# Running the last 64 rows of two products in pairs on the two halves of the partitions, with biases added by ScalarE and GpSimd

## The chip, the cores and the metric

One core of a Trainium2 chip runs the kernel. TensorE multiplies matrices into PSUM banks, VectorE, ScalarE and GpSimd (DVE, ACT and POOL in the profile) work on rows of 128 partitions, and SyncE (SP) issues the DMA transfers. The metric is the device time of one execution in microseconds.

## What is computed

Input x has 8 batches of 512 tokens of 576 numbers, all f32. A first layer rotates x in a 64-dimensional subspace; a second is one transformer block whose attention runs over the 16 heads of one token, and whose shifts, scales and gates come from a condition vector of each batch.

```
x = x + ((x U) R - x U) U^T                    # U from a QR, R = expm of a skew matrix
shift_a, scale_a, gate_a, shift_m, scale_m, gate_m = split(silu(c) @ ada_w + ada_b, 6)
h = layernorm(x) * (1 + scale_a) + shift_a
q, k, v = split((h @ qkv_w + qkv_b), 3)        # 576 -> 3 * 576; per token 16 heads of 36
att = softmax(q k^T / 6) v                     # 16 x 16 scores for each token
x = x + gate_a * (reshape(transpose(att)) @ proj_w + proj_b)
h = layernorm(x) * (1 + scale_m) + shift_m
x = x + gate_m * (gelu(h @ fc1_w + fc1_b) @ fc2_w + fc2_b)      # 576 -> 2304 -> 576
```

## The kernel before

A preparation stage (about 240 us, its order written out by hand) makes U by a QR on VectorE, the rotation by a matrix exponential on TensorE and GpSimd, and the modulation tables. The exponential's products (`products`, L367) take 64x64 blocks alternately from partitions 0-63 and 64-127. `mod` holds shift and scale with features on partitions.

The main part goes over 17 units of the tokens: two of one 128-token tile and 15 of two tiles. A contraction over 576 features is cut into chunks of 128, 128, 128, 128 and 64 rows (`KROWS`). The last chunk has a 65th row: `xn`, the normed tile, is padded with a column of ones (`padded`, L577), which transposed becomes a row of ones, and the weights carry the bias as row 576. `srows(c)` is 65 for the last chunk. So the query product and fc1 get their bias inside the last matmul.

- `normed` (L600): layer norm on VectorE, with the root taken by GpSimd (L610).
- `feature_major` (L663) and `Projection.turn_normed` (L803): TensorE transposes normed tiles; ScalarE scales and shifts them on the way out of PSUM into `hT` or `h2T` (L675, L814).
- `qkv` (L685): for a token tile, four groups of 432 columns, five chunks each, into one bank of the pool `ps_mm` (two banks); ScalarE copies each group to `tok` (L703).
- `attention` (L708): VectorE multiplies (L721, L743) and sums (L727, L749) per four heads; ScalarE takes the exponential.
- `Projection.product` (L786): attention's output by proj_w into `ps_mm`; VectorE multiplies by the gate and so frees the bank (L795, `pt`), then adds.
- `norm` (L798): normed again, then GpSimd adds `gb2` (gate_m times fc2's bias, made once a batch at L1007 from `b2`, which stays in SBUF) to the tile (L801).
- `fc1` (L829): for group g of 9, two blocks k of 128 hidden features. Each has its own weight tile w1 (320 KB, pool `wst`, ring of 4) and five chunks (L838) into one half of a bank of `ps_f1` (two banks). One gelu takes the whole bank (L846).
- `mlp` (L907): fc2 by a Strassen-like scheme with seven products instead of eight. GpSimd makes sums of gelu's output (L923 to L926), weights come from `in_fc_q` (wq) and from combinations made during the first batch (`comb_d`, wt). Its matmuls are at L938 to L943, one product left for the end at L953. The first batch uses `mlp_plain` (L893).

In the unit loop (from L1000), the queries of unit k+1 are issued during unit k: three groups, then the turn of attention's output, then the fourth group, the projection, the second tile's groups, the turn of the normed tile, then the MLP. In a batch's second unit the next batch's rotation is set between fc1 groups (`aside`); it begins with `gps` (L631), a 64-row product. In fc1's loop fc2 runs one group behind: fc1(g), fc2(g-1), fc1(g+1). At a batch's first unit `gate_rows` (L597) loads the gates by DMA.

Outside the preparation a scheduler orders the instructions of each engine at compile time by its own estimate of when each is ready; each engine and SP then works its list in order.

Of the kernel before, what the change touches and what calls it, by code (L numbers as in the profile page):

```python
# [9 lines left out]
F32 = mybir.dt.float32  # L10
# [38 lines left out]
def rotate_then_dit_block(  # L49
# [7 lines left out]
    qkv_w: bass.AP,  # L57
    proj_w: bass.AP,
    fc1_w: bass.AP,
    fc2_w: bass.AP,  # L60
    fc2_q: bass.AP,
    fc2_b: bass.AP,
# [5 lines left out]
    def load_rows(dst, src, tail):  # L68

        nc.sync.dma_start(out=dst[:, 0:4], in_=src[0:512].rearrange("(c p) n -> p c n", p=128))  # L70
        nc.sync.dma_start(out=dst[0:tail, 4], in_=src[512 : 512 + tail])
# [22 lines left out]
    nc.gpsimd.memset(u[R:, 4, 0:R], 0.0)  # L94
    fmi = const.tile([128, B // 2, R], F32, tag="fmi", name="fmi")
    mod = const.tile([128, 4, NK, B], F32, tag="mod", name="mod")
    b2 = const.tile([128, D], F32, tag="b2", name="b2")

    wqkv = const.tile([128, NK, 3 * D], F32, tag="wqkv", name="wqkv")

    t3 = const.tile([128, NP, HALF], F32, tag="t3", name="t3")

    def srows(c):
        return 65 if c == 4 else 128


    for i in range(4):
        nc.gpsimd.memset(mod[64:65, i, 4, :], float(i % 2))


    xin = ctx.enter_context(tc.tile_pool(name="xin", bufs=1))
# [2 lines left out]
    with tc.manual_schedule(engines=engines), tc.tile_pool(name="prep", bufs=1) as prep, tc.tile_pool(name="qrs", bufs=2) as qrs, tc.tile_pool(  # L114
# [202 lines left out]
        def modulation(v):  # L317
            ps = ps_m.tile([128, NK, B], F32, tag="m", name=f"mod_{v}")
            for c, rows in enumerate(KROWS):
                first = v * D + c * 128  # L320
                nc.tensor.matmul(
                    ps[0:rows, c], lhsT=ada_rows[:, first : first + rows], rhs=ident[0:B, 0:B], start=True, stop=True
                )
            for c0, c1, rows in ((0, 4, 128), (4, 5, 64)):
                dst = mod[0:rows, v // 3 * 2 + v % 3, c0:c1, :]
                if v % 3:
                    nc.scalar.activation(dst, ps[0:rows, c0:c1], AF.Identity, bias=ones[0:rows, 0:1])
                else:
                    nc.scalar.copy(dst, ps[0:rows, c0:c1])


        wr = prep.tile([128, NK, NSKEW], F32, tag="wr", name="wr")
# [142 lines left out]
        for j in range(R):  # L475
            t, done = qr_step(j, t, done)
            if j > 1:
                next(side, None)
            if j == 8:
                load_rows(wqkv, qkv_w, 65)  # L480
                nc.sync.dma_start(out=b2, in_=fc2_b.to_broadcast([128, D]))
                for g in (6, 7, 8):
                    load_ada(g)
        for _ in side:
# [92 lines left out]
    def padded(tag, n):  # L577
        out = []
        for k in range(n):
            t = big.tile([128, NK * 128], F32, tag=f"{tag}{k}", name=f"{tag}{k}")  # L580
            nc.gpsimd.memset(t[:, D:], 0.0)
            nc.gpsimd.memset(t[:, D : D + 1], 1.0)
            out.append(t)
        return out

    xns = padded("xn", 5)
    ats = padded("at", 2)
    turn = {"xn": 0, "at": 0}

# [10 lines left out]
    def normed(xt, name):  # L600

        st = small.tile([128, 2, 6], F32, tag="st", name=f"st_{name}")
        mv = small.tile([128, 2], F32, tag="mv", name=f"mv_{name}")
        rs = small.tile([128, 1], F32, tag="rstd", name=f"rstd_{name}")
        xn = take("xn", xns)
        for n in range(2):
            nc.vector.bn_stats(st[:, n, :], xt[:, n * HALF : (n + 1) * HALF])
        nc.vector.bn_aggr(mv, st)
        nc.vector.tensor_scalar(rs, mv[:, 1:2], LN_EPS, None, ALU.add)  # L609
        nc.gpsimd.tensor_tensor(rs, rs, mhalf[:, 0:1], ALU.pow)  # L610
        nc.vector.tensor_scalar(xn[:, 0:D], xt, mv[:, 0:1], rs, ALU.subtract, ALU.mult)
        return xn

    hTs = {}
# [48 lines left out]
    def feature_major(b, half):  # L663

        if half == 0:
            hTs[b] = big.tile([128, NK, S], F32, tag="hT", name=f"hT_{b}")
        hT = hTs[b]

        pair = normed_x.pop((b, half))
        for c in range(NK):  # L670
            rows = srows(c)
            ps = ps_mm.tile([128, 2, 128], F32, tag="mm", name=f"htr_{b}_{half}_{c}")
            for t in range(2):
                nc.tensor.transpose(ps[:, t, :], pair[t][:, c * 128 : (c + 1) * 128], ident)
            nc.scalar.activation(  # L675
                hT[0:rows, c, half * 256 : half * 256 + 256],
                ps[0:rows].rearrange("p t s -> p (t s)"),
                AF.Identity,
                bias=mod[0:rows, 0, c, b : b + 1],
                scale=mod[0:rows, 1, c, b : b + 1],  # L680
            )

    toks = {}
# [1 line left out]
    def qkv(b, i):  # L685


        hT = hTs[b]
        tok = tiles.tile([128, 3 * D], F32, tag="qkv", name=f"qkv_{b}_{i}", bufs=3)
        N = 3 * D // 4  # L690

        def group(n):
            ps = ps_mm.tile([128, N], F32, tag="mm", name=f"qkvp_{b}_{i}_{n}")
            for c in range(NK):
                k = srows(c)
                nc.tensor.matmul(  # L696
                    ps,
                    lhsT=hT[0:k, c, i * 128 : (i + 1) * 128],
                    rhs=wqkv[0:k, c, n * N : (n + 1) * N],
                    start=c == 0,  # L700
                    stop=c == NK - 1,
                )
            nc.scalar.copy(tok[:, n * N : (n + 1) * N], ps)  # L703

        toks[b, i] = tok
        return [lambda n=n: group(n) for n in range(4)]

    def attention(b, ts):  # L708
# [3 lines left out]
        NU = len(ts)  # L712
        hb = f"{b}_{ts[0]}"
        own = [toks.pop((b, i)) for i in ts]
        sc2 = small.tile([128, 2, H, H], F32, tag="sc", name=f"sc_{hb}", bufs=2)[:, 0:NU]
        for t, tok in enumerate(own):
            q = tok[:, 0:D].rearrange("p (h d) -> p h d", d=DH)
            k = tok[:, D : 2 * D].rearrange("p (h d) -> p h d", d=DH)
# [37 lines left out]
    class Projection:  # L756
# [46 lines left out]
        def turn_normed(self, cs):  # L803

            if cs[0] == 0:
                self.h2T = tiles.tile([128, NK, 256], F32, tag="h2T", name=f"h2T_{self.hb}", bufs=1)
            b, tokens = self.b, len(self.ts) * 128
            ps = ps_f1.tile([128, 2, 2, 128], F32, tag="f1", name=f"h2tr_{self.hb}_{cs[0]}")
            for k, c in enumerate(cs):
                for t in range(len(self.ts)):  # L810
                    nc.tensor.transpose(ps[:, k, t, :], self.xn[t][:, c * 128 : (c + 1) * 128], ident)
            for k, c in enumerate(cs):
                rows = srows(c)
                nc.scalar.activation(  # L814
                    self.h2T[0:rows, c, 0:tokens],
                    ps[0:rows, k].rearrange("p t s -> p (t s)")[:, 0:tokens],
                    AF.Identity,
                    bias=mod[0:rows, 2, c, b : b + 1],
                    scale=mod[0:rows, 3, c, b : b + 1],
                )  # L820


# [5 lines left out]

    def fc1(pr, g):  # L829

        hb, h2T, NU = pr.hb, pr.h2T, len(pr.ts)
        ps = ps_f1.tile([128, 2, NU * 128], F32, tag="f1", name=f"fc1_{hb}_{g}")
        for k in range(2):
            w1 = wst.tile([128, NK, 128], F32, tag="w1", name=f"w1_{hb}_{g}_{k}")
            nc.sync.dma_start(out=w1, in_=fc1_w[2 * g + k])
            for c in range(NK):
                n = srows(c)
                nc.tensor.matmul(  # L838
                    ps[:, k],
                    lhsT=w1[0:n, c, :],  # L840
                    rhs=h2T[0:n, c, 0 : NU * 128],
                    start=c == 0,
                    stop=c == NK - 1,
                )
        gt = tiles.tile([128, 2, NU, 128], F32, tag="gt", name=f"gt_{hb}_{g}", bufs=3)
        nc.scalar.activation(gt.rearrange("p k t s -> p (k t s)"), ps.rearrange("p k s -> p (k s)"), AF.Gelu)  # L846
        return gt

    def finish(hb, t, n, made, gate):
# [139 lines left out]
    def now(pieces):  # L989
        for piece in pieces:  # L990
            piece()
# [11 lines left out]
    for k, (b, ts) in enumerate(units):  # L1003
        if ts[0] == 0:
            gate_a, gate_m = gate_rows(0, b), gate_rows(1, b)
            gb2 = big.tile([128, D], F32, tag="gb2", name=f"gb2_{b}")
            nc.gpsimd.tensor_tensor(gb2, gate_m, b2, ALU.mult)  # L1007

        pr = Projection(b, ts, gate_a)
        if k == 0:  # L1010
# [5 lines left out]
            q = qkv(nb, nts[0]) + qkv(nb, nts[1])  # L1016
        if len(ts) == 1:
            pr.turn(0)
            now(q[:1])
            pr.product(0, 0)  # L1020
            pr.product(0, 1)
            pr.norm(0, gb2)
            now(q[1:3])
            pr.turn_normed((0, 1))
            now(q[3:])
        else:
            now(q[:3] if k > 2 else q)
            pr.turn(0)
            now(q[3:4] if k > 2 else [])
            pr.product(0, 0)  # L1030
            pr.turn(1)
            pr.product(0, 1)
            pr.norm(0, gb2)
            pr.product(1, 0)
            pr.product(1, 1)
            pr.norm(1, gb2)
            now(q[4:7] if k > 2 else [])
            pr.turn_normed((0, 1))
            now(q[7:] if k > 2 else [])
# [64 lines left out]
```

## Time and profile before

| | us |
|---|---|
| median of 3 runs (2232.11 to 2236.47) | 2233.76 |
| profiled execution | 2228.81 |
| its span, first to last instruction | 2227.0 |
| preparation, up to | 240 |
| a steady unit of two tiles (1203 to 1320) | 117 |
| TensorE, VectorE busy in it | 116.5, 95.3 |
| fc1 group, two tiles (20 matmuls) | 4.32 |

PE is the matmuls, PEld the weight loads. A group of instructions in the profile is a line, an engine, an operation, its tiles and form, a count, then busy time, mean ns of one, and idle time before them with what ended it. A timeline row is start, length, engine, line, operation, tiles, form and count; neighbours of one kind are merged. Successive matmuls overlap in the records, since the end of each is modelled: what one costs is the step from its start to the next one's. SPq rows are DMA issues.

### The profile page before, as it was taken

The numbers are of one execution on the slowest core, as the hardware profiler recorded it, in microseconds if no ns is written. First come the engines' busy times: TensorE is split into PE (matmuls) and PEld (weight loads), VectorE is DVE, ScalarE is ACT, GpSimd is POOL, SyncE is SP. The second block draws the span as 40 slices with busy tenths as digits, with TensorE's granted clock in tenths as the row PEclk, the third lists the DMA queues.
The fourth block names the chain that finished last, engine by engine and source line by source line (L and its number), as shares of the span: only waits on it lengthen the run. The fifth ranks groups of instructions, "written<-read, shape, count | busy, mean of one in ns | idle before, by whom it ended". The sixth has DMA issues, their size and how long they took to land.

```text
span 2227.0 us, 26157 instructions
## 1 busy us (share of the span) xinstructions
PE 2104.2 (94%) x9571; PEld 1570.8 (71%) x9571; DVE 1789.4 (80%) x2443; ACT 386.7 (17%) x817; POOL 679.6 (31%) x846
## 2 busy tenths in 40 slices
PE   7788879899799999999999999999999999999998
PEld 3485437666568686868687777777786868686877
DVE  8997399899678797969796979697988889697930
ACT  2232111122021111111111112121211122111110
POOL 2151000113434242424242433324332334242422
PEclk9755789999999999999999999999999999999999
DMA  9101116743647373845565465637373737364654
GB/s 304 30 2 62 50 54 206 249 124 111 186 156 233 107 214 108 251 128 170 155 201 165 153 178 168 205 116 208 128 231 98 215 114 225 111 202 122 200 178 125
DMA packets 211698, 347.58 MB, mean 156 GB/s; under 512 B 82382, under 2 KB 100123, under 8 KB 211572
## 3 DMA queue, kind: packets, MB, share of 16 engines
q1 hardware_dynamic: 211572, 345.92, 51.3%
q8 instruction: 77, 1.26, 0.2%
q14 instruction: 49, 0.40, 0.1%
HBM read 313.46 MB, written 32.39 MB: 155 GB/s over the span
## 4 chain that ended last, share of the span: by engine, by line
PE 65%; DVE 14%; issue 11%; DMA 6%; POOL 3%; ACT 1%; SPq 0%; POOLq 0%; DVEq 0%; ACTq 0%
PE fc L838 26%; PE fc L938 8%; PE qkvp L696 7%; PE fc L943 5%; DVE sc L727 3%; PE fc L940 3%; PE p L953 3%; DMA w<-in_fc_w 3%; PE fc L893 2%; PE ada L310 2%; DMA out<-x 1%; DVE qk L721 1%; PE zps L640 1%; DVE pv L743 1%; DVE att L749 1%
## 5 line engine op out<-in xcount | busy, mean ns | idle before, releaser
L838 PE MATMUL fc<-h2T,w 128*128 128x256 f32 (+3 forms) x3060 | 656.4, 368 | 2.0 <-ACT h2T L814 1.9
L838 PEld LDWEIGHTS fc<-h2T,w 128*128 128x128 f32 (+1 forms) x3060 | 549.4, 191 | 76.8 <-ACT h2T L814 7.0
L696 PE MATMUL qkvp<-wqkv,hT 128*128 128x432 f32 (+1 forms) x1280 | 480.9, 529 | 1.3 <-DVE pt L795 0.9
L721 DVE TENSOR_TENSOR qk<-qkv 128x2304 f32<-128x2304 f32 x128 | 327.3, 2557 | 122.9 <-ACT qkv L703 120.4
L696 PEld LDWEIGHTS qkvp<-wqkv,hT 128*128 128x128 f32 (+1 forms) x1280 | 240.6, 191 | 204.5 <-issue 196.4
L743 DVE TENSOR_TENSOR pv<-sc,qkv 128x2304 f32<-128x2304 f32 x128 | 330.9, 2585 | 3.3
L749 DVE TENSOR_REDUCE att<-pv 128x144 f32<-128x2304 f32 x128 | 326.5, 2551 | 3.3
L727 DVE TENSOR_REDUCE sc<-qk 128x64 f32<-128x2304 f32 x128 | 326.3, 2549 | 2.8
L923 POOL TENSOR_TENSOR ss<-gt 128x128 f32<-128x128 f32 x126 | 135.1, 1072 | 539.4 <-ACT gt L846 539.4
L846 ACT ACTIVATE gt<-fc 128x512 f32<-128x512 f32 (+1 forms) x153 | 87.5, 572 | 725.2 <-PE fc L838 725.0
L703 ACT COPY qkv<-qkvp 128x432 f32<-128x432 f32 x128 | 66.3, 518 | 559.0 <-PE qkvp L696 552.6
L943 PEld LDWEIGHTS fc<-wt,ss 128*128 128x128 f32 x1008 | 140.5, 190 | 13.2
L943 PE MATMUL fc<-wt,ss 128*128 128x144 f32 x1008 | 144.1, 286 | 0.0
L938 PE MATMUL fc<-wq,gt 128*128 128x288 f32 x504 | 142.8, 405 | 0.0
L610 POOL TENSOR_TENSOR rstd_m<-rstd_m,mhalf 128x1 f32<-128x1 f32 x32 | 17.6, 551 | 362.0 <-DVE rstd_m L609 338.3
L969 DVE TENSOR_TENSOR u<-u,fc 128x288 f32<-128x288 f32 x14 | 6.4, 454 | 135.3 <-ACT u L968 135.3
L793 PE MATMUL pj<-w2q_p,aT 128*128 128x288 f32 x384 | 108.5, 419 | 4.0 <-DMA w2q_p<-in_proj_w 2.3
L938 PEld LDWEIGHTS fc<-wq,gt 128*128 128x128 f32 x504 | 94.1, 189 | 19.9
L854 POOL TENSOR_TENSOR x<-x,mt 128x288 f32<-128x288 f32 x64 | 50.8, 796 | 169.5 <-DVE mt L853 169.5
L893 PE MATMUL fc<-w,gt 128*128 128x288 f32 x288 | 82.6, 431 | 20.4 <-DMA w<-in_fc_w 19.8
L925 POOL TENSOR_TENSOR ss<-gt,ss 128x128 f32<-128x128 f32 x126 | 97.7, 776 | 9.9
L793 PEld LDWEIGHTS pj<-w2q_p,aT 128*128 128x128 f32 x384 | 71.7, 194 | 31.5 <-issue 6.2
(223 smaller groups left out, 2381.1 us busy)
## 6 DMA issues: line engine op xcount, KB each, us to landing
w<-in_fc_w SPq DMA_DIRECT2D x306, 320.0 KB, 3.4
wq<-in_fc_q SPq DMA_DIRECT2D x126, 432.0 KB, 3.7
wt<-comb_d SPq DMA_DIRECT2D x126, 432.0 KB, 4.2
w<-in_fc_w SPq DMA_DIRECT2D x54, 288.0 KB, 4.1
w2q_p<-in_proj_w SPq DMA_DIRECT2D x34, 432.0 KB, 3.7
xT<-in_x_t SPq DMA_DIRECT2D x16, 640.0 KB, 10.1
w2t_p<-in_proj_w SPq DMA_DIRECT2D x34, 288.0 KB, 3.3
xt<-in_x SPq DMA_DIRECT2D x32, 288.0 KB, 2.8
```

Source lines behind the costliest of these rows:

```text
L696: nc.tensor.matmul(ps, lhsT=hT[0:k, c, i * 128 : (i + 1) * 128], rhs=wqkv[0:k, c, n * N : (n + 1) * N], start=c == 0, stop=c == NK - 1,)
L721: nc.vector.tensor_tensor(pr, q[:, c * HC : (c + 1) * HC].unsqueeze(2).to_broadcast([128, HC, H, DH]), k.unsqueeze(1).to_broadcast([128, H ...
L727: nc.vector.tensor_reduce(sc2[:, t, c * HC : (c + 1) * HC, :], pr, AX.X, ALU.add)
L743: nc.vector.tensor_tensor(pr, sc2[:, t, c * HC : (c + 1) * HC, :].unsqueeze(2).to_broadcast([128, HC, DH, H]), v.unsqueeze(1).to_broadcast ...
L749: nc.vector.tensor_reduce(att[:, c * HC : (c + 1) * HC, :], pr, AX.X, ALU.add)
L793: nc.tensor.matmul(ps, lhsT=aT[0:k, c, :], rhs=w, start=c == 0, stop=c == NK - 1)
L838: nc.tensor.matmul(ps[:, k], lhsT=w1[0:n, c, :], rhs=h2T[0:n, c, 0 : NU * 128], start=c == 0, stop=c == NK - 1,)
L893: nc.tensor.matmul(acc[t, n][:, 0:HALF], lhsT=gts[g][:, k, t], rhs=w2[k][:, n * HALF : (n + 1) * HALF], start=g + k == 0, stop=g == NP - 1 ...
L923: nc.gpsimd.tensor_tensor(ss[:, 0], gt[:, 0, 1], gt[:, 1, 1], ALU.add)
L925: nc.gpsimd.tensor_tensor(ss[:, 2], gt[:, 1, 0], ss[:, 1], ALU.subtract)
L938: nc.tensor.matmul(p[k], lhsT=whole[k][0], rhs=whole[k][1], start=g == 0, stop=stop)
L943: nc.tensor.matmul(bank[:, side], lhsT=lhs, rhs=rhs[:, n * QUARTER : (n + 1) * QUARTER], start=False, stop=stop, skip_group_check=True,)
```

## The change

Rows 512 to 575, the last chunk, lie once on partitions 0-63 and once on 64-127, and two products of 64 rows that follow each other use one half each.

- In the layer norm, xn is 640 wide with columns 512 to 575 copied to 576 to 639 by ScalarE; there are no ones. The transposes give the last chunk on both halves, and `mod` is filled on both halves (`modulation` makes its last chunk's matmul twice).
- `qkv`: groups 0 and 2 take both `ps_mm` banks and end with a pair: their own tail on one half of the partitions, and the next group's tail on the other, which starts that group's sum. Groups 1 and 3 have four chunks left. ScalarE's copy is followed by an addition of the bias by GpSimd.
- `fc1`: the tail of block 1 of group g runs beside that of block 0 of group g+1, whose weights and bank are taken at the end of group g. Group 0's first tail and group 8's last run alone. Both tails of a pair come in one weight tile, and block 1 of groups 0 to 7 loads four chunks (256 KB) instead of five. Gelu runs once per block with the bias as its per-partition operand.
- `gb2` is made from a load of fc2's bias in each batch; the ring of xn has four tiles instead of five, and that of the scores one instead of two.

```diff
+    def tail_rows(n):
+        return slice(n % 2 * 64, n % 2 * 64 + 64)
...
+        nc.scalar.copy(xn[:, D:], xn[:, 512:D])
...
         def group(n):
-            ps = ps_mm.tile([128, N], F32, tag="mm", name=f"qkvp_{b}_{i}_{n}")
-            for c in range(NK):
-                k = srows(c)
...
-            nc.scalar.copy(tok[:, n * N : (n + 1) * N], ps)
+            odd = n % 2 == 1
+            if not odd:
+                for k in (n, n + 1):
+                    held[k] = ps_mm.tile([128, GN], F32, tag="mm", name=f"qkvp_{b}_{i}_{k}")
+            for c in range(4):
+                product(n, c, slice(0, 128), c == 0 and not odd, c == 3 and odd)
+            if not odd:
+                product(n, 4, tail_rows(n), False, True)
+                product(n + 1, 4, tail_rows(n + 1), True, False)
+            cols = slice(n * GN, (n + 1) * GN)
+            nc.scalar.copy(tok[:, cols], held.pop(n))
+            nc.gpsimd.tensor_tensor(tok[:, cols], tok[:, cols], bqkv[:, cols], ALU.add)
...
-        sc2 = small.tile([128, 2, H, H], F32, tag="sc", name=f"sc_{hb}", bufs=2)[:, 0:NU]
+        sc2 = small.tile([128, 2, H, H], F32, tag="sc", name=f"sc_{hb}", bufs=1)[:, 0:NU]
...
     def fc1(pr, g):
...
+        def pair(g):
+            pr.w1 = [wst.tile([128, NK, 128], F32, tag="w1", name=f"w1_{hb}_{g}_{k}") for k in range(2)]
+            for k, w1 in enumerate(pr.w1):
+                n = NK if k == 0 or g == NP - 1 else 4
+                nc.sync.dma_start(out=w1[:, 0:n], in_=fc1_w[2 * g + k][:, 0:n])
+            pr.bank = ps_f1.tile([128, 2, NU * 128], F32, tag="f1", name=f"fc1_{hb}_{g}")
...
+        here, there, whole = tail_rows(g), tail_rows(g + 1), slice(0, 128)
+        if g == 0:
+            pair(0)
+            product(pr.bank, 0, pr.w1[0], 4, here, start=True)
+        ps, w1 = pr.bank, pr.w1
         for k in range(2):
...
+            for c in range(4):
+                product(ps, k, w1[k], c, whole, stop=k == 0 and c == 3)
+        if g + 1 < NP:
+            pair(g + 1)
+            product(ps, 1, pr.w1[0], 4, here, stop=True)
+            product(pr.bank, 0, pr.w1[0], 4, there, start=True)
+        else:
+            product(ps, 1, w1[1], 4, here, stop=True)
         gt = tiles.tile([128, 2, NU, 128], F32, tag="gt", name=f"gt_{hb}_{g}", bufs=3)
-        nc.scalar.activation(gt.rearrange("p k t s -> p (k t s)"), ps.rearrange("p k s -> p (k s)"), AF.Gelu)
+        for k in range(2):
+            nc.scalar.activation(
+                gt[:, k].rearrange("p t s -> p (t s)"), ps[:, k], AF.Gelu, bias=b1[:, 2 * g + k : 2 * g + k + 1]
+            )
...
-            nc.gpsimd.tensor_tensor(gb2, gate_m, b2, ALU.mult)
+            nc.sync.dma_start(out=gb2, in_=fc2_b.to_broadcast([128, D]))
+            nc.gpsimd.tensor_tensor(gb2, gate_m, gb2, ALU.mult)
```

## The prediction

> **What bounds the kernel now.** I read the busy shares of the page first, then a table of busy time by stretch, one unit of two token tiles to a stretch.
>
> ```profile
> PE 2104.2 (94%) x9571; PEld 1570.8 (71%) x9571; DVE 1789.4 (80%) x2443; ACT 386.7 (17%) x817; POOL 679.6 (31%) x846
> ...
> 1085.00:1203.00 118.00, 117.53 (x527) 90.63 (x526) 103.31 (x97) 22.43 (x42) 44.29 (x49) 1.00 0.60 183
> 1203.00:1320.00 117.00, 116.54 (x499) 87.48 (x498) 95.28 (x69) 17.98 (x32) 37.26 (x44) 1.00 0.52 155
> ```
>
> In a steady unit TensorE is busy 117.5 of 118 us at full clock, VectorE 95 to 103. So TensorE sets the unit's length, VectorE has 14 to 22 us of idle time, ScalarE and GpSimd have plenty. Next the matmul groups with shapes kept apart; in the chain that ended last, 20 of them take 4.32 us, 216 ns each.
>
> ```profile
> L838 PE MATMUL fc<-h2T,w 128*128 128x256 f32 x2160 | 517.3, 380 | 1.1 <-ACT h2T L814 1.1
> ...
> L838 PE MATMUL fc<-h2T,w 65*128 65x256 f32 x540 | 161.7, 380 | 0.0
> L696 PE MATMUL qkvp<-wqkv,hT 65*128 65x432 f32 x256 | 113.9, 526 | 0.0
> ```
>
> The 65-row products are what the change pairs. The program has half as many as the counts say: every f32 product appears as two matmuls, each with its own weight load. What counts is the step from one start to the next: 216 ns (256 columns; 220 after a 65-row one), 362 ns (432 columns; 367), 112 ns (128 columns). Four tail matmuls (two products) cost 0.872 us in fc1 and 1.458 in the query product.
>
> Do two halves run at once, and what does entering that mode cost? The timeline of TensorE shows both, for smaller tiles. In the matrix exponential, products alternate between partitions 0-63 and 64-127. Sixteen matmuls start from 124.10 to 124.86, in pairs 7 ns apart, 107 ns from pair to pair; ten of one shape on one tile (L496) start singly 107 ns apart. So halves do overlap there, each with both its passes. The projection of the rotation shows the way in and out:
>
> ```profile
> 1351.77 0.82 PE L811 MATMUL h2tr<-ident,xn 128*128 128x128 f32 x6
> 1352.52 1.18 PE L631 MATMUL gps<-ut,fmi 64*64 64x288 f32 x4
> 1353.63 4.59 PE L838 MATMUL fc<-h2T,w 128*128 128x256 f32 x20
> ```
>
> The last transpose starts at 1352.317, the first 64-row matmul at 1352.519: 202 ns where 109 is the step, 93 too many. To the second it is 294 where 242 is the step: its weights (64 columns, 52 ns) are loaded in the open. From the last 64-row one to the first whole one it is 332 instead of 242 (+90), and to the second whole one 320 instead of 216 (+104, a load of 128 columns in the open). All six rotations repeat this within 2 ns.
>
> **The change part by part.** *The pairs.* A pair needs 128-column loads, so I take 107 for the load on entry (L549, 64 rows by 128 columns, shows 102 to 107 from load to matmul). One visit to the half mode costs 93 + 107 + 90 + 104 = 394 ns. This row speaks against a rule of the Trainium skill: "TensorE: Matmul & The Clock Gate", Part 3, gives a pack of tiles the duration of one matmul plus about 4 ns per further tile, with no price for the visit; "TensorEngine Tiling (Array Packing)", Key Properties, says that changing the mode drains the engine, without a figure. Call the price of a visit s.
> - fc1, 15 units of two tiles: nine groups with 18 tails make 8 pairs and two tails alone (group 0's first, group 8's last). 120 pairs: 872 - (2 x 216 + 7) = 433 ns saved each, less s. 30 single ones: 436 - 432 = 4 ns saved, less s.
> - queries: 32 token tiles, two pairs each, 64 pairs: 1458 - (2 x 362 + 7) = 727 ns saved, less s.
> - Sum: 52.0 + 0.1 + 46.5 = 98.6 us, less 214 visits x s. By the span rule (s = 0) 98.6 us; by the row (394 ns, 84.3 us) 14.3 us. fc1 alone loses 7.0, the queries gain 21.3. I take the row: it is this chip and this type. Bounds: s between 0 and 500 (were the second half's load not beside the first's, 107 more).
> - The two units of one tile: 16 pairs at 224 + 7 + 394 - 448 = +177 and 4 single +394: +4.4 us. These stretches move 260 GB/s at 0.84 DMA share, and the change drops 64 KB of every second w1 (8 of 18): 1 MB, 4 us at that rate. I take zero, -4 to +4.4.
>
> *w1 earlier.* Group g+1's weights are now needed at the end of group g's products instead of at g+1's start, some 2.9 us (fc2) earlier. Now a w1 is issued about 12 us before use (1256.42 for the group at 1268.56) and lands in 3.4, so 4 to 5 us of cover stay; zero. On SP's queue it moves ahead of wq and wt (432 KB each, 3.7 and 4.2 us to landing), which are used a group later. Gone, the cover would cost each group its shortfall, 1 us each making 135.
>
> *Gelu in two.* An activation of 128x512 takes 0.60, of 128x256 with bias 0.46 to 0.55: +0.3 us per group. GpSimd's sums wait for it, but TensorE uses them some 6 us later: zero (153 groups x 0.3 = 46 us if it didn't). The tail copy on ScalarE in each layer norm (64 columns) is below the 0.37 us of a 256-column copy, wanted only by the last transpose, behind four others: zero (at most 0.4 for each of 64 norms).
>
> *GpSimd's bias.* 128 additions of 128x432. GpSimd took 0.80 us for 128x288 and 1.55 for 128x576, so 1.18 each; beside a VectorE product it stretches:
>
> ```profile
> 1227.91 1.55 POOL L801 TENSOR_TENSOR x<-x,gb 128x576 f32<-128x576 f32 x1 [0.69 <-DVE xn L611]
> ...
> 1237.13 3.66 POOL L801 TENSOR_TENSOR x<-x,gb 128x576 f32<-128x576 f32 x1 [2.46 <-DVE xn L611]
> ```
>
> That is up to 151 us open, some 300 covered, on an engine with 70% idle. "SBUF — State Buffer", Who interferes with whom, calls the shared port an exclusive lock, so VectorE may wait too: at most 8 x 1.18 = 9.4 us a unit; the longest product at L721 was 3.09 against a median of 2.557, so I take half, hidden in its 14 us.
>
> Latency is not hidden. VectorE's attention starts right after the third copy (wait L721 <- ACT L703, 120.4 us over 14 units). It now waits an addition more, 1.2 us. Behind it on VectorE stand the gate products (L795) that free the two ps_mm banks for TensorE. Worse is what is ahead on GpSimd. Every second unit opens a batch:
>
> ```profile
> 1314.96 0.80 POOL L854 TENSOR_TENSOR x<-x,mt 128x288 f32<-128x288 f32 x1 [0.39 <-DVE mt L853]
> 1322.52 3.54 POOL L1007 TENSOR_TENSOR gb<-gate,b 128x576 f32<-128x576 f32 x1 [6.77 <-DMA gate<-gates_d]
> ```
>
> The gate lands 10 us after the unit's first query product (1312.06), because SP stands behind a store until 1318. gb2's product is ahead of the queries in the program; if additions two and three stay behind it, attention starts at 1322.5 + 1.55 + 2 x 1.18 + 0.1 = 1326.5 instead of 1322.24. VectorE then runs product and sum (5.1) and the gate product (0.45), and frees the first bank at 1332.1. TensorE wants it at 1330.4 (1331.08 before, less two pairs' 0.33 each): 1.7 lost, and some 0.5 at the next bank. I take 2.2 us for each of seven such units (15.4; 0 to 35 if all of the delay reaches TensorE), 0.4 for the seven others (2.8), 1.5 at the start, where the first attention is waited for in the open, and 2 in all for the norms whose rstd (L610) queues behind an addition. Sum 21.7, bounds 0 and 45.
>
> *The rest.* gb2's own load (288 KB per batch) lands beside the gate's; a ring of 4 instead of 5 normed tiles comes round after their transposes; one score buffer suffices since attentions follow each other on VectorE; the bias loads and 8-row matmuls of the preparation lie under its VectorE chain. If that cover went, some 4 us once. Zero.
>
> **The sum.** The profiled execution took 2228.8 us (span 2227.0). -14.3 + 21.7 = +7.4. The median of the runs is 5.0 above the profiled one, so 2233.8 + 7.4 = 2241.
>
> **Rivals.**
> 1. *The visit is cheap* (not slower; chance 0.25): only rows, not columns, change in this mode, and no row here shows that. If loads hide and only the drains (93 + 90 = 183) stay: 98.6 - 39.2 = 59.4, less 21.7: 2196. It decides from s below (98.6 - 21.7) / 0.214 = 359 ns.
> 2. *Full price, no new waits* (0.15): the order on GpSimd and VectorE puts additions before gb2's product; 2 us are left: 2233.8 - 12.3 = 2221.
> 3. *The halves don't overlap* (0.13): the trace shows it only where columns differ too. A pair then costs 4 whole steps and a visit: 120 x 386 + 30 x 390 + 64 x 384 ns = 82.6, plus 21.7: 2338.
>
> My own case has 0.47, with 2230 to 2262 by its bounds. Faster by over 0.2% (4.5 us, about what a measurement can tell from no change) takes rivals 1 and 2 and a little of my own: 0.41; within it 0.13; slower 0.46. The range leaves out rival 3 and the cheapest end of rival 1: 2190 to 2272.
>
> **What would show it.** In the timeline, tails of 64 rows start in pairs 7 ns apart; the step into them is about 93 longer, the one after 90. A group of fc1 takes 3.46 + 0.83 us instead of 4.32. L721 waits for L703's GpSimd addition, longer in units that open a batch; waits of pj on L795 grow. A visit below 359 ns, or VectorE's start unmoved, proves me wrong towards faster; single steps of 216 among the tails, towards slower.

## The result and the profile after

The changed kernel takes 2298.39 us, median of 4 runs (2290.03 to 2306.27); the kernel before took 2232.94 beside it (2222.89 to 2236.47). The ratio of the means is 1.030 (1.025 to 1.035): slower by about 67 us, where 7 had been forecast. The profiled execution took 2306.27 us with a span of 2304.5, 77.5 more than before.

First the page's busy line and, from the groups by shape, the 64-row products of fc1 and GpSimd's additions (busy time, mean ns of one, idle before).

```profile
PE 2122.6 (92%) x9579; PEld 1487.8 (65%) x9579; DVE 1814.4 (79%) x2443; ACT 439.1 (19%) x1030; POOL 818.8 (36%) x960
```

```profile
L866 PE MATMUL fc<-h2T,w 64*128 64x256 f32 x540 | 106.3, 431 | 10.3 <-DMA w<-in_fc_w 6.9 <-ACT h2T L836 3.4
...
L726 POOL TENSOR_TENSOR qkv<-qkv,bqkv 128x432 f32<-128x432 f32 x128 | 173.2, 1358 | 182.6 <-ACT qkv L725 182.6
```

TensorE's share of busy time fell from 94% to 92% of a longer span: time was lost to waits. An addition took 1.36 us on average, inside the bounds of 1.18 and 2.4.

The pairs did what was forecast. In the records of the steady group that begins at 1287.06, sixteen whole matmuls start 216 ns apart; the step into the 64-row ones is 309 (93 more), the two of a pair start 7 ns apart, and the step out is 306 (90 more). One period of fc1 and fc2 went from 7.24 us (1261.31 to 1268.56 before) to 7.20 (1287.06 to 1294.27): 40 ns gained where 433 - 394 = 39 had been forecast.

The loss shows in two successive units, the first of which opens a batch (start and end, length, busy time and count of TensorE, its weight loads, VectorE, ScalarE and GpSimd, then the clock granted to TensorE, the DMA share and GB/s).

```profile
1097.50:1230.50 133.00, 123.70 (x539) 87.77 (x538) 105.53 (x97) 27.08 (x59) 50.56 (x57) 0.97 0.54 164
1230.50:1344.80 114.30, 111.75 (x488) 78.59 (x487) 96.32 (x69) 19.70 (x41) 47.55 (x52) 1.00 0.51 151
```

Cut at their first query products, the same units took 122.5 and 112.9 before. The unit that opens a batch is 10.5 longer and its granted clock is 0.97; the other is 1.4 longer. GpSimd's, VectorE's and TensorE's timelines in the opening unit tell why:

```profile
1101.19 1.09 POOL L726 TENSOR_TENSOR qkv<-qkv,bqkv 128x432 f32<-128x432 f32 x1
1110.32 1.41 POOL L1055 TENSOR_TENSOR gb<-gate,gb 128x576 f32<-128x576 f32 x1 [8.03 <-DMA gate<-gates_d]
1111.68 3.21 POOL L726 TENSOR_TENSOR qkv<-qkv,bqkv 128x432 f32<-128x432 f32 x3
```

```profile
1113.87 3.44 DVE L744 TENSOR_TENSOR qk<-qkv 128x2304 f32<-128x2304 f32 x1 [13.50 <-POOL qkv L726]
1117.34 2.55 DVE L750 TENSOR_REDUCE sc<-qk 128x64 f32<-128x2304 f32 x1
1119.92 2.56 DVE L744 TENSOR_TENSOR qk<-qkv 128x2304 f32<-128x2304 f32 x1
1122.40 0.45 DVE L818 TENSOR_TENSOR pt<-pj,gate 128x288 f32<-128x288 f32 x1
```

```profile
1114.87 1.14 PE L816 MATMUL pj<-w2t_p,aT 128*128 128x288 f32 x4
1122.99 3.22 PE L816 MATMUL pj<-w2q_p,aT 128*128 128x288 f32 x6 [6.99 <-DVE pt L818]
1126.00 2.08 PE L816 MATMUL pj<-w2t_p,aT 128*128 128x288 f32 x4
1127.92 1.62 PE L816 MATMUL pj<-w2q_p,aT 128*128 128x288 f32 x6
```

The first addition runs at once; the next ones stand behind gb2's product, which waits 8 us for the gate's DMA. Attention starts 16.3 us into the unit instead of 10.2. Ahead of the gate product that frees TensorE's bank VectorE has three operations (product, sum, product), 8.5 us with the first stretched from 2.56 to 3.44 beside the last addition. TensorE stands for 7 us, and after that the same six matmuls take 3.22 us instead of 1.62: the stall also costs clock.

That stall is not the only one. Later in the unit the rotation's product `zps` waits for VectorE. The wait is 1.89 us in five of the six opening units of the steady part (the last batch has no rotation after it), and in four of them the clock is halved behind it, here in the first row and not in the second:

```profile
925.12 3.29 PE L653 MATMUL zps<-xT,u 128*128 128x256 f32 x10 [1.89 <-DVE xt L669]
1174.02 2.42 PE L653 MATMUL zps<-xT,u 128*128 128x256 f32 x10 [1.89 <-DVE xt L669]
```

The clock column behind the first of these waits, behind the 7 us stall and behind the second wait:

```profile
926.50:929.90 3.40, 3.40 (x9) 2.64 (x8) 3.40 (x3) 0.37 (x1) 0.00 (x0) 0.50 0.22 78
1121.10:1127.90 6.80, 4.91 (x10) 3.53 (x11) 5.67 (x7) 0.00 (x0) 0.00 (x0) 0.50 0.09 17
1174.00:1177.40 3.40, 3.38 (x16) 2.99 (x17) 3.40 (x4) 0.37 (x1) 1.25 (x3) 1.00 0.30 105
```

### The profile page after: what moved, and what is told of

Same layout as the page of the kernel before. It is cut to its first block, busy times and chain, and to the rows that moved or that the text cites. A ratio compares the mean times of both kernels' runs of the same rounds, so it can differ in the third digit from the quotient of the medians.

```text
span 2304.5 us, 26335 instructions
## 1 busy us (share of the span) xinstructions
PE 2122.6 (92%) x9579; PEld 1487.8 (65%) x9579; DVE 1814.4 (79%) x2443; ACT 439.1 (19%) x1030; POOL 818.8 (36%) x960
## 4 chain that ended last, share of the span: by engine, by line
PE 61%; DVE 20%; issue 7%; DMA 5%; POOL 5%; ACT 1%; SPq 1%; POOLq 0%; DVEq 0%; ACTq 0%
PE fc L866 20%; PE qkvp L706 10%; PE fc L985 7%; DVE qk L744 5%; PE fc L990 5%; DVE sc L750 4%; PE pj L816 3%; PE p L1000 2%; DVE pv L766 2%; PE fc L987 2%; PE fc L940 2%; DMA w<-in_fc_w 2%; POOL qkv L726 2%; DVE att L772 2%; DMA out<-x 1%
## 5 line engine op out<-in xcount | busy, mean ns | idle before, releaser
L866 PE MATMUL fc<-h2T,w 128*128 128x256 f32 (+3 forms) x3060 | 644.4, 382 | 14.4 <-DMA w<-in_fc_w 10.4
L866 PEld LDWEIGHTS fc<-h2T,w 128*128 128x128 f32 (+1 forms) x3060 | 495.1, 192 | 134.0 <-issue 52.4
L744 DVE TENSOR_TENSOR qk<-qkv 128x2304 f32<-128x2304 f32 x128 | 340.3, 2659 | 166.7 <-POOL qkv L726 164.1
L706 PE MATMUL qkvp<-wqkv,hT 128*128 128x432 f32 (+1 forms) x1280 | 456.4, 544 | 0.4 <-DVE xt L669 0.2
L706 PEld LDWEIGHTS qkvp<-wqkv,hT 128*128 128x128 f32 (+1 forms) x1280 | 209.8, 191 | 207.8 <-issue 203.4
L973 POOL TENSOR_TENSOR s<-gt 128x128 f32<-128x128 f32 x126 | 115.7, 919 | 520.2 <-ACT gt L891 519.4
L891 ACT ACTIVATE gt<-fc,b 128x256 f32<-128x256 f32 (+1 forms) x306 | 124.4, 458 | 621.2 <-PE fc L866 600.3
L726 POOL TENSOR_TENSOR qkv<-qkv,bqkv 128x432 f32<-128x432 f32 x128 | 173.2, 1358 | 182.6 <-ACT qkv L725 182.6
L816 PE MATMUL pj<-w2q_p,aT 128*128 128x288 f32 x384 | 116.7, 444 | 47.4 <-DVE pt L818 43.7
L985 PE MATMUL fc<-wq,gt 128*128 128x288 f32 x504 | 154.5, 429 | 0.0
L990 PEld LDWEIGHTS fc<-wt,ss 128*128 128x128 f32 x1008 | 140.5, 190 | 13.2
L971 POOL TENSOR_TENSOR ss<-ss,gt 128x128 f32<-128x128 f32 x126 | 97.8, 776 | 9.9
```

The lines of the kernel that those rows point to most:

```text
L706: nc.tensor.matmul(held[n], lhsT=hT[rows, c, i * 128 : (i + 1) * 128], rhs=wqkv[rows, c, n * GN : (n + 1) * GN], start=start, stop=stop,)
L726: nc.gpsimd.tensor_tensor(tok[:, cols], tok[:, cols], bqkv[:, cols], ALU.add)
L744: nc.vector.tensor_tensor(pr, q[:, c * HC : (c + 1) * HC].unsqueeze(2).to_broadcast([128, HC, H, DH]), k.unsqueeze(1).to_broadcast([128, H ...
L816: nc.tensor.matmul(ps, lhsT=aT[0:k, c, :], rhs=w, start=c == 0, stop=c == NK - 1)
L866: nc.tensor.matmul(bank[:, k], lhsT=w1[rows, c, :], rhs=h2T[rows, c, own], start=start, stop=stop, skip_group_check=True,)
L891: nc.scalar.activation(gt[:, k].rearrange("p t s -> p (t s)"), ps[:, k], AF.Gelu, bias=b1[:, 2 * g + k : 2 * g + k + 1])
```

## Experiments

The theory after the traces, **Q**: the order on GpSimd, gb2's product ahead of the additions, makes most of the loss. Its rivals in the first four runs: **L**, the additions cost this whatever stands ahead of them; **V**, visits or pairs cost more than 394 ns. (In the later runs V stands for another theory, told there.) Each time stands beside runs of the kernel before on the same chip, and losses and gains are taken from the ratios.

**e1, gb2's product behind the additions.**

```
-            nc.gpsimd.tensor_tensor(gb2, gate_m, gb2, ALU.mult)
+            if k < 3:
+                nc.gpsimd.tensor_tensor(gb2, gate_m, gb2, ALU.mult)
...
             now(q[3:4] if k > 2 else [])
+            if k > 2 and ts[0] == 0:
+                with tc.issue_after(added[-1].ins):
+                    nc.gpsimd.tensor_tensor(gb2, gate_m, gb2, ALU.mult)
```

> The changed kernel, with gb2's product on GpSimd put behind the first tile's four additions in every unit that opens a batch. Theory Q (the queue: the loss is attention starting late because additions two to four stand behind gb2's product, which waits for the gate's DMA): those seven units become like the others, which lost 2.8 us against 9, so about 45 us come back: 2250 us (2235 to 2262), and the 7 us waits of pj on VectorE are gone. Theory L (latency: the addition itself and the port that GpSimd shares with VectorE cost the time in every unit): at most 10 us come back, 2288 or more. Theory V (visits: entering and leaving the half mode costs more than pairs save): no change, 2298.

Measured 2254.02 (before 2225.24): ratio 1.0121 (1.0084 to 1.0159). In its trace gb2's product follows the fourth addition at once:

```profile
1105.14 1.10 POOL L727 TENSOR_TENSOR qkv<-qkv,bqkv 128x432 f32<-128x432 f32 x1 [2.51 <-ACT qkv L726]
1106.20 1.42 POOL L1082 TENSOR_TENSOR gb<-gate,gb 128x576 f32<-128x576 f32 x1
```

About 40 of the 67 us are the order on GpSimd. L and V fall as the main cause; 27 us of loss stay, 20 more than my sum.

**e2, no additions.** The line with the addition is left out, and with it the biases.

> The changed kernel without the 128 additions on GpSimd; the queries' bias is left out of the computation. Theories Q and L both: nothing stands between ScalarE's copy and attention, so what is left is the products' gain of 14 us and some ordering: 2222 us (2210 to 2238). Theory V: the pairs still cost, 2260 or more. The difference to the kernel with gb2's product behind is what the additions cost by themselves: Q expects 10 to 30 us, L nearly all of the loss.

Measured 2232.37: 1.0029 (1.0005 to 1.0053). Another 20 us were the additions. But with no waits of GpSimd left the pairs should have shown their 14 us, and it is 7 slower than before. This run opened the second question.

**e3, the kernel before with additions and gb2's reload,** nothing paired; the rings of four normed tiles and one score buffer are as in the change.

```
+            nc.gpsimd.tensor_tensor(tok[:, cols], tok[:, cols], bqkv[:, cols], ALU.add)
...
-            nc.gpsimd.tensor_tensor(gb2, gate_m, b2, ALU.mult)
+            nc.sync.dma_start(out=gb2, in_=fc2_b.to_broadcast([128, D]))
+            nc.gpsimd.tensor_tensor(gb2, gate_m, gb2, ALU.mult)
```

> The kernel before, unpaired, with row 576 of the query weights zero and the bias added by GpSimd as in the change; gb2 reloaded per batch, four normed tiles and one score buffer as in the change. Only the pairs, the gelu bias and fc1's order are missing. Theory Q: the whole loss of waits without the pairs' gain: 2233 + 85 = 2318 us (2300 to 2330), slower than the change itself, with 7 us waits of pj in units that open a batch. Theory V: near before, 2235 to 2250.

Measured 2288.68: 1.0293 (1.0255 to 1.0331), a miss. The loss is there without any pair, as Q says, but undoing the pairs costs nothing: in the full change they are worth no time that can be measured. The ledger below says why.

**e4, both tails on rows 0 to 63,** so that halves cannot overlap.

```
-        return slice(n % 2 * 64, n % 2 * 64 + 64)
+        return slice(0, 64)
```

> The changed kernel with both tails of each pair on partitions 0 to 63, so that they run one after the other in the half mode; the weights of fc1's two tails then overwrite each other in the packed tile, so fc1's last 64 rows are wrong weights, with the same instructions. If halves overlap as the timeline of the change shows (7 ns between starts), the overlap was worth 52 us in fc1 and 46.5 in the queries, so 2298 + 98 = 2396 us, or 2360 where waits hide part. If they didn't overlap, 2298.

Measured 2328.37: 1.0474 (1.0428 to 1.0521). The overlap is real (tails now start 216 and 363 ns apart), but losing it costs some 40 us and not 98: with slower products TensorE's wait for the gate products shrinks from 43.7 to 17.1 us over the whole trace. TensorE's own time and the kernel's time are two things here.

**A ledger of the steady units.** So I separated them. The stretch is 12 units, six of which open a batch: from the first query product of the first of them to the first projection product of the last unit. From it I take TensorE's waits for other engines in that stretch; the rest is TensorE's own time. Before:

```profile
PE h2tr L811 <- DVE xn L611: 5.5, 12, 0.5
PE fc L838 <- ACT h2T L814: 0.9, 1, 0.9
PE pj L793 <- DVE pt L795: 0.4, 1, 0.4
```

in the changed kernel, two of four items (engine, line and what it waited for; us in total, times, longest):

```profile
PE pj L816 <- DVE pt L818: 43.2, 18, 7.0
PE zps L653 <- DVE xt L669: 9.4, 5, 1.9
```

and in e2 (before and here an item of 0.2 is left off):

```profile
PE h2tr L833 <- DVE xn L622: 14.1, 12, 1.2
PE pj L815 <- DVE pt L817: 5.2, 12, 0.4
PE fc L865 <- ACT h2T L835: 2.5, 6, 1.3
```

The last column is what a halved clock cost: half of the time that TensorE worked where the clock column shows 0.50 in the stretch.

| kernel | stretch | waits | TensorE's own | of it halved clock |
|---|---|---|---|---|
| before | 1402.5 | 7.0 | 1395.5 | 0 |
| after | 1468.0 | 62.6 | 1405.4 | 19 |
| e1 | 1419.7 | 33.0 | 1386.7 | 0 |
| e2 | 1406.5 | 22.0 | 1384.5 | 0 |
| e3 | 1461.5 | 46.3 | 1415.2 | 18 |
| e4 | 1482.6 | 19.6 | 1463.0 | 3 |
| f1, queries' pairs only | 1400.5 | 21.4 | 1379.1 | 0 |
| f2, fc1's pairs only | 1408.0 | 8.4 | 1399.6 | 0 |
| h1, before with both edits to VectorE's list | 1403.7 | 8.9 | 1394.8 | 0 |
| h4, queries' pairs with both edits | 1396.0 | 18.4 | 1377.6 | 0 |

Without the halved clock the pairs take 11 us off TensorE's time between e3 and the changed kernel (1397 to 1386), and 16 us come back as waits. Losing the overlap in e4 adds 74 (1386 to 1460; by the prices 96 x 425 + 48 x 717 ns = 75), and waits fall by 43.

In e2 TensorE's own time fell by 11.0; by my prices it is 48 x 333 ns for the queries plus 96 x 39 less 24 x 390 ns for fc1, together 10.4. The price was right, and 15 us came back as waits, most of them for VectorE: for the second norm, and for the gate products. VectorE's timeline before shows the reason:

```profile
1210.87 2.56 DVE L721 TENSOR_TENSOR qk<-qkv 128x2304 f32<-128x2304 f32 x1 [8.81 <-ACT qkv L703]
1213.47 2.55 DVE L727 TENSOR_REDUCE sc<-qk 128x64 f32<-128x2304 f32 x1
1216.05 2.56 DVE L721 TENSOR_TENSOR qk<-qkv 128x2304 f32<-128x2304 f32 x1
1218.53 0.45 DVE L795 TENSOR_TENSOR pt<-pj,gate 128x288 f32<-128x288 f32 x1
...
1234.01 2.55 DVE L727 TENSOR_REDUCE sc<-qk 128x64 f32<-128x2304 f32 x1
1236.48 0.57 DVE L611 TENSOR_SCALAR xn<-x,mv_m,rstd_m 128x576 f32<-128x576 f32 x1
```

From the third query copy to the second norm, 26 us, VectorE works off a list with one gap of 0.30 us. Its long idle time in this part of the unit (8.81 us here) lies ahead of that list, where it waits for the queries. TensorE transposes the second tile's norm, which comes at the end of the list. That is theory **V** of the next runs: VectorE sets the stretch from the third query copy to fc1's start. With pairs the third copy comes 11.50 us after the first query product instead of 11.64, so all that the pairs can give is 0.14 us a unit. Theory **S**: TensorE sets it, and the missing us lie in the pairs.

**f1, only the queries paired; f2, only fc1 paired.** The product left unpaired runs its last chunk over all 128 rows, with zeros below; the queries' biases are left out of both. f1, and f2's query product:

```
-            for c in range(4):
-                product(ps, k, w1[k], c, whole, stop=k == 0 and c == 3)
+            for c in range(NK):
+                product(ps, k, w1[k], c, whole, start=c == 0, stop=c == NK - 1)
```

```
+            for c in range(NK):
+                product(n, c, slice(0, 128), c == 0, c == NK - 1)
```

> Only the queries' products are paired; fc1's tails run unpaired, over all 128 rows with zeros below; the queries' biases are left out, so GpSimd adds nothing. Theory V: from the first query product to the first fc1 matmul of a unit the path runs over VectorE (third query copy, attention's first products, gate products, norms), and the third copy comes only 0.14 us earlier with pairs; 14 x 0.14 = 2 us faster than before, so within 2217 to 2228 where before has 2225. Theory S: TensorE sets that stretch too, and the 21 us missing in the run without additions lie in fc1 or in dearer visits: then the queries' 64 pairs bring their 21.3 us and it is 2204 (below 2210).

> Only fc1 is paired; the queries' tails run unpaired over 128 rows with zeros below, and their biases are left out. Theory V: the queries' pairs were worth nothing, so this is as the run without additions, 2232 (2228 to 2237): fc1's units of two tiles cost 7.0 by the price of 394 ns (4 to 7), the units of one tile up to 6 more. Theory S: it loses the 21.3 us of the queries' pairs against that run, 2253 (above 2246).

Measured f1 2219.3, ratio 0.9972 (0.9952 to 0.9991), 6 us faster of the 21; f2 2232.37, 1.0044 (1.0012 to 1.0076). V holds, S falls: fc1's pairs alone give the same ratio as both within the intervals. In the ledger f1 takes 16.4 us off TensorE's own time (48 x 333 ns = 16.0) and adds 14.4 of waits; f2 adds 4.1 (priced 5.6).

**f3 and f5, attention starts a group earlier.** The columns of the query weights are put in the order half of q, k, other half of q, v; attention's first two products then need two groups instead of three.

```
-        "qkv_w": np.concatenate([qkv_w[:, : 2 * D], v_w.reshape(D + 1, D)], axis=1),
+        "qkv_w": np.concatenate([qkv_w[:, 0:HALF], qkv_w[:, D : 2 * D], qkv_w[:, HALF:D], v_w.reshape(D + 1, D)], axis=1),
```

> Queries paired, fc1 unpaired over 128 rows, additions kept, gb2's product behind them, and the columns of the query weights put in the order half of q, k, other half of q, v, so that attention's first two products need two groups of columns instead of three. Theory V: attention can start some 4.0 us earlier (a group of 2.9 and a pair of 1.1), which pays the addition of 1.2 and uncovers TensorE's own time: 2225 less the queries' 21 and less the waits that before had in this stretch (some 0.7 a unit, 10 in all), 2194 at best; 2195 to 2212. If the start of attention doesn't set the stretch, or if its first products only go in front of the gate products, it isn't below 2219.

> The kernel before with nothing but that order of columns: attention starts up to 3.6 us earlier, TensorE's work is unchanged. Theory V: the waits in the stretch up to fc1 go, some 0.7 us in each of 14 units, 10 in all: 2215 (2210 to 2221 where before has 2225). Theory S: 2225 (2222 to 2228).

Measured f3 2242.36, 1.0086 (1.0059 to 1.0113), a miss; f5 2221.31, 0.9973 (0.9945 to 1.0), between its two theories. f5's steady units are together not shorter (112.6 and 123.1 us against 112.8 and 122.5); it gains ahead of them (the first begins at 725.6 instead of 728.0). In f3 attention does start at 8.85 us of a unit instead of f1's 11.50, but fc1 still starts at 43.16 (f1: 43.12): the list only got longer at its front. And it ends in new waits, in the opening units for the rotation's step on VectorE:

```profile
PE zps L653 <- DVE xt L669: 14.9, 5, 3.0
PE qkvp L707 <- DVE pt L819: 14.6, 12, 1.2
```

So V is too narrow: it is the order and length of VectorE's list that decide, not where it starts.

**g1 to g4, the norm ahead of attention's third and fourth product.**

```
+                behind = t == 0 and c > 1 and (b, ts[0]) > (1, 0)
+                with tc.issue_after(last["m"].ins) if behind else nullcontext():
```

> The kernel before, with VectorE's list cut: attention's third and fourth products of its first tile (and their sums behind them, 10.2 us) are issued after the unit's second norm instead of among its steps. Theory V (VectorE works off a list without a gap from the third query copy to the second norm, and TensorE waits at its end): TensorE's waits in that stretch go, 0.7 us a unit and 10 in all, 2215 where before has 2225 (2208 to 2220). If VectorE is short of time in the unit as a whole, the 10 us come back as waits for attention: 2230 or more.

> The run with only the queries paired (fc1 unpaired over 128 rows, biases left out), with VectorE's list cut in the same way. Theory V: now nothing stands between the pairs and the end of the stretch, so they bring the 21.3 us by the price of 394 ns that they did not bring with the list uncut: 21 below the kernel before with the same cut, 2194 (2187 to 2202). Theory S' (the pairs themselves save less than the steps say): no more than 6 below it, 2209 or more.

> The same with the biases added by GpSimd and gb2's product behind the additions: the whole reference is computed. Theory V: an addition more before attention starts, 1.2 us a unit, which VectorE's shorter list now covers in part; 5 us at the start in the open: 2199 if it is all covered, 2216 if none is.

> The whole change, fc1's pairs too, with gb2's product behind the additions and VectorE's list cut. Theory V: the kernel with only the queries paired plus fc1's price, 4 us in the two-tile units and 6 in the one-tile units: 10 above it, so 2209 to 2226.

Measured g1 2230.09 (before 2222.33), 1.0014 (0.9996 to 1.0033); g4 2228.57, 1.0028 (1.0006 to 1.0051); g2 2249.1, 1.012 (1.0054 to 1.0186); g3 2267.31, 1.0187 (1.014 to 1.0234). All four missed; g1's time is the one that its expectation named for a VectorE short of time. In g1 the waits for the norm went as expected and fc1 starts 0.68 us sooner in nearly every unit, but the opening units are longer behind that point (83.0 us from fc1's start to the next unit instead of 80.9), and in the last unit TensorE waits 1.7 us for attention's output. g4's time is where its expectation put S', but its ledger refutes S': against g1 TensorE's own time fell by 13.4 (1394.6 to 1381.2), and waits rose by 12.0. They tell where the pairs' gain went this time:

```profile
PE zps L654 <- DVE xt L670: 12.6, 5, 2.5
PE pj L818 <- DVE pt L820: 5.2, 12, 0.4
```

The work taken out of the list stands in front of the rotation's step in the opening units, and TensorE waits there. In an opening unit of the kernel before (1076.7 to 1199.2) VectorE stands for 7.4 us ahead of attention and 7.3 near the unit's end; between them no gap is longer than 0.9.

**h1, h4 and h2, both edits:** f5's order of columns, and only the fourth product behind the norm (c > 2).

> The kernel before with two edits: the columns of the query weights reordered, so that attention starts after two groups of columns (3.6 us earlier in VectorE's idle time), and attention's fourth product of the first tile issued after the second norm. Theory V' (VectorE has no time to spare from the third query copy to the rotation's steps; the cut alone gave back 0.7 us a unit at the second norm and lost 2.1 in each opening unit): with 3.6 us more for VectorE both hold, 2215 where before has 2225 (2205 to 2220). Otherwise 2223 or more.

> The same two edits in the kernel with only the queries paired (fc1 unpaired over 128 rows, biases left out). Theory V': the pairs bring most of 4 x 333 ns a unit, 19 in all: 19 below the run of before with both edits, 2196 (2188 to 2205). Theory S' (the pairs don't save what the steps say): 6 or less below it, 2209 or more.

> The same with the biases added by GpSimd, gb2's product behind them: the whole reference is computed. Theory V': the additions' 1.2 us a unit are covered by the earlier start, 5 us at the start are not: 2201 (2193 to 2212), faster than the kernel before. If they are not covered: 2218 or more.

Measured h1 2216.01 (before 2227.03), 0.9965 (0.9945 to 0.9985); h4 2207.58, 0.9927 (0.9906 to 0.9947); h2 2241.3, 1.0074 (1.0052 to 1.0096). h1 has the expected time for another reason: its steady stretch isn't shorter (1403.7 against 1402.5); it gains at the start, where the first attentions are waited for in the open (its first steady unit begins at 721.4 instead of 728.0, from the same start of the first query product, 257). h4 lies between the theories. The ledger settles it: against h1 TensorE's own time fell by 17.2 us (priced 16.0), the stretch by 7.7, and waits rose by 9.5:

```profile
PE qkvp L707 <- DVE pt L820: 10.2, 12, 1.2
PE zps L654 <- DVE xt L670: 6.9, 5, 1.4
```

The pairs save what their steps say; about half comes through once VectorE has 3.6 us more. h2 shows that the additions are not covered even then. Its ledger has 14.6 and 12.7 us of waits for the gate products and the rotation's step. f1 and h4, the faster ones with pairs, leave the queries' biases out. Of the kernels that compute the whole reference only h1 is clearly faster than the kernel before, and it has no pairs; f5's interval reaches 1.0.

## Why the prediction was wrong

**Right:** the steps in and out (93 and 90), the overlap (7 ns), the price of 394 ns, "fc1 alone loses 7.0" (f2: 9.8 by the ratio, 6.2 by the medians, 4.1 in 12 units by the ledger), the mechanism at gb2's product, and which units it hits. Rival 3 (the halves don't overlap) and rival 1 (the visit is cheap) were refuted by the steps. Rival 2 asked for what e1 made, additions ahead of gb2's product; it would have given 2221, e1 gave 2254. Two readings are a little off without moving the sum: the sixteen matmuls of the exponential start up to 124.91, not 124.86, and they, like L549's loads, ran where the clock was 0.50; in the changed kernel the load on entry is 104 ns (97 in the step, plus 7) where 107 was taken. The bounds 0 and 45 of the loss would give 2219 to 2265, not 2230 to 2262.

**"I take 2.2 us for each of seven such units": the term that was mis-sized most.** An opening unit is 8.6 us longer in the changed kernel than in e1 (five of them, 131.6 to 133.7, against 124.0). Four parts were missed. I counted one product and sum ahead of the gate product, 5.1 us; the timeline before already has three operations there:

```profile
1322.24 2.56 DVE L721 TENSOR_TENSOR qk<-qkv 128x2304 f32<-128x2304 f32 x1 [7.36 <-ACT qkv L703]
1324.84 2.55 DVE L727 TENSOR_REDUCE sc<-qk 128x64 f32<-128x2304 f32 x1
1327.42 2.56 DVE L721 TENSOR_TENSOR qk<-qkv 128x2304 f32<-128x2304 f32 x1
1329.90 0.45 DVE L795 TENSOR_TENSOR pt<-pj,gate 128x288 f32<-128x288 f32 x1
```

With these 7.66 us the same sum would have freed the bank at 1334.6 and lost 4.2 + 0.5 us. Attention came 3.8 to 6.1 us late in six units (4.9 on average, near the 4.3), and its product was stretched by 0.9. And the stall was priced as a stall alone: the halved clock after it costs 2.5 us more in the ten matmuls shown. The Trainium skill says as much of a long stall ("TensorE: Matmul & The Clock Gate", Part 1: an array idle for a window of some 3.4 us falls to half rate until it has been busy for about as long); the trace has half speed for 4.9 us after 7.0 of standing. But it also has it for 3.4 us after waits of 1.89, in four units of five, and there the measurement decides: my 2.2 us, too, could have met a halved clock. The fourth part is that wait of 1.89 us ahead of `zps`, which neither e1 nor the kernel before has in these units.

Together they fit: in the unit from 1097.54 TensorE waits 9.3 us, in e1's same unit 2.8, and the halved clock costs 2.5; that makes 9.0, and the unit is 8.9 longer. Over the stretch the halved clock costs 19 us by the clock column, and TensorE's own time differs by 18.7 between the changed kernel and e1.

**"0.4 for the seven others."** e1 against e2 has 1.1 us in each of the units, opening or not (124.0 against 122.9, 114.2 against 113.1): one addition of 1.10 us and its hand-over, whole. The step that failed is "TensorE sets the unit's length, VectorE has 14 to 22 us of idle time": the long idle time is ahead of attention, and behind it attention's later start by 1.1 us reached TensorE whole.

**"Sum: 14.3 us."** The same step failed for the gain. TensorE's own time fell as summed, but 15 of e2's us returned as waits at the end of VectorE's list. I counted the queries' pairs as on the path because TensorE was busy 117.5 of 118 us; it had waited only 0.6 us a unit, and most of that little wait was already VectorE's list ending last. In e2 that wait, for the second norm, grew from at most 0.5 to 1.2 us a unit, and one of 0.4 for the gate products joined it: two engines ended close together, and shortening one showed the other.

**Small items.** The units of one tile were taken at zero (-4 to +4.4). From the first query product to the second such unit's projection e2 takes 6.2 us longer (144.0 against 137.8), the changed kernel 8.1 (145.9). That is most of the 12 us by which its profiled span grew outside the steady stretch (8.2 ahead of it, 3.8 behind). What makes it so was not separated.

**The account.** Of the 65.5 us in the changed kernel's 12 steady units, e2 has 4.0, the additions 13.2 (e1 less e2), gb2's order 48.3 (after less e1, waits 29.6 and TensorE's own time 18.7). For the last the prediction had 15.4 in seven such units, their additions included. By the ratios the three are about 7, 20 and 40. That the halved clock makes the whole 18.7 is worked out from the clock column, not isolated by a run. Open is also what would let the other half of the queries' pairs through: a VectorE list short enough to end ahead of TensorE in opening units was not reached.

## What to carry to other kernels

A busy share near 100% names the engine whose time is filled, not the only one on the path: before counting a saving on it, look for where it waits even for half a us each period, and follow the other engine's list back to its last gap; here a saving was worth little more than the distance to that list (f1: 2.0 us of 16.4 in the steady units). An operation added to hand-overs between engines cost its whole duration here (1.1 us a unit), since the receiver works off its list without a gap, and it inherited the wait that stood ahead of it in its own queue. Count what is queued ahead of the releasing instruction in the timeline, operation by operation.

## What the runs showed of the hardware

In the changed kernel's steady stretch the clock is halved ten times, for 3.4 or 6.8 us each: behind each of the six waits for the gate product, 4.7 to 7.0 us long, and behind four of five waits of 1.89 us. Waits up to 1.4 us, as in e1 and h4, left it at 1.00, and so did five waits of 1.8 us in g1; of five waits of 2.55 us in h2 three were followed by a halved clock. So length alone does not tell, between 1.8 and 3 us.

A VectorE product that began while the last of three additions ran on GpSimd, with 1.0 us of it left, took 3.44 us instead of 2.56. A visit to the half-array mode cost the same in both products, about 393 ns, and a pair's two matmuls start 7 ns apart on halves with the same columns. The kernel's first query product starts at 247 us in some profiled executions and at 257 in others (257.0 in before, 247.5 in g1, whose edit comes later), so single spans differ by 10 us for no reason of the change, which is why the ledger leaves the start out.
